# One layer of a four-layer network: from one engine in written order to four, with its works cut into half-unit steps

## The chip, the core and the metric

The kernel runs on one core of a Trainium2 chip. The metric is the device time of one execution in microseconds; the number compared is the median of several runs. The engines are named as in the profile: PE (TensorE, matrix multiplication), DVE (VectorE), ACT (ScalarE), POOL (GpSimd) and SP (the queue that issues transfers). PSUM is the memory that PE writes its results to, in eight banks of 512 float32 per partition. SBUF is the working memory.

## The reference

The reference is a network of four layers over an activation of 8 x 512 x 128 float32. Each layer normalizes `x`, computes a sequence part `s` and a feed-forward part `g`, and adds `s * silu(g)`. Only layer 3 matters here. Its two parts, shortened:

```python
xn = _layernorm(x)
# sequence part: a state-space layer with 4 heads of 64, state size 128
z, x, Bg, Cg, dd_dt, dd_A, trap, angles = split(u @ W_in)
dt = softplus(dd_dt + dt_bias);  adt = min(-softplus(dd_A), -1e-4) * dt
theta = cumsum(angles * dt)
K = rope(rmsnorm(Bg) * B_norm_w + B_bias, theta)
Q = rope(rmsnorm(Cg) * C_norm_w + C_bias, theta)
# chunk by chunk: masked Q K^T with decay, times x; plus a state that is carried on
y = (y_intra + y_inter + D * x) * silu(z)
s = y @ W_out
# feed-forward part: attention of 16 heads of 8, softmax over the queries
scores = einsum('bqd,bkd->bkq', q, k) / sqrt(128)
z = einsum('bkq,bkv->bqv', softmax(scores, -1), v) @ Wo
g = gelu(l2_normalize(l2_normalize(z) @ Wff))
x = x + s * silu(g)
```

## The kernel before

The four layers run one after the other. `x` stays in SBUF. Layer 3 (`layer3`, L1971, and the class `Layer3`, L1593) takes the eight rows of the batch one by one; a row is 512 tokens, that is `JT` = 4 tiles of 128 tokens. Four kinds of work exist for each row, and all but the attention are generators, which are advanced one step at a time up to their next `yield`:

- **A start** (`begin`, L1663, and `parameters`, L1701): normalizes the row (`layernorm`, `rms`), transposes it, projects keys (L1682), queries (L1685, four masked copies at L1688 and L1690) and values (L1694), and then computes everything the state-space part needs for each token: raw B and C and the small parameters (L1713 to L1719), a softplus as a polynomial of some 15 small DVE operations (L1581 to L1590), decays (L1747, L1749), the normalized B and C (L1759), the products of B and C (L1763 to L1774), the angles (L1778 to L1792), sine and cosine (L1795 to L1798).
- **Four mixers** (`mixer`, L1802), one for each tile of 128 tokens: projection of z and x (L1808 to L1814), keys and queries with bias on POOL (L1817), rotation on DVE (L1822 to L1824), the decay matrix (L1829, L1834, masked by POOL at L192), transposes (L1848), the product of keys and queries (L1853, L1854), the carried state (L1859 to L1865), the output (L1870 to L1879), and a transpose of it (L1883, L1884).
- **Sixteen units of attention**: `scores` (L1907) computes four heads for one tile of keys: four matmuls into four PSUM tiles of one bank each (L1916), and for each head a maximum on DVE (L1919) and an exponential with a running sum on ACT (L1920). `weigh` (L1887), two units later (`LAG` = 2), divides the values by the sums (L1893 on DVE, L1894 on POOL) and multiplies them with the exponentials on PE (L1901).
- **A closing** (`end`, L1922): output projections (L1929, L1939), two normalizations, a projection between them (L1955), GELU (L1959) and tanh (L1962), the last products and sum (L1963 to L1966), and one output transfer (L1967).

The loop in `layer3` goes over units. In each unit it issues the scores, advances half of the running works by one step, issues the weighing of two units before, and advances the other half by one step. So each work advances one step per unit. The start of the next row begins at unit 0, a mixer every four units (four units ahead of the row it belongs to), and the closing after the last weighing.

What sets the order: PE executes in the order in which the program is written (`manual_schedule` with PE alone). For DVE, ACT and POOL a scheduler chooses the order from its own estimate of the times and from priorities; `scores` and `weigh` have a higher priority by 300. On every engine the order is fixed once the program is built. Most copies out of PSUM go alternately to ACT and DVE (`evac`, L116 to L122). PSUM holds four banks for scores (`pu`), one for the weighing (`pf`) and three for everything else (`pa`).

Of the kernel before, what the change touches and what calls it, by code (L numbers as in the profile page):

```python
# [20 lines left out]
P = 128  # L21
B = 8
# [1551 lines left out]
def softplus(nc, pool, x):  # L1574
# [5 lines left out]
    nc.scalar.activation(e, e, AF.Exp, scale=-1.0)  # L1580
    nc.vector.tensor_scalar(z, e, 2.0, None, ALU.add)  # L1581
# [11 lines left out]
class Layer3:  # L1593
# [43 lines left out]
    def layernorm(self, x, xn):  # L1637

        k, nc = self.k, self.k.nc
        s1 = self.sp2.tile([P, JT], F32, name="s1")  # L1640
        nc.vector.tensor_reduce(s1, x, AX.X, ALU.add)
        nc.vector.tensor_scalar(s1, s1, 1.0 / C, None, ALU.mult)
        nc.vector.tensor_tensor(xn, x, bc(s1, 2, C), ALU.subtract)
        r = self.rms(xn, JT, 1e-5)
        nc.vector.tensor_tensor(xn, xn, bc(r, 2, C), ALU.mult)

    def rms(self, x, n, eps, floor=False):


        nc = self.k.nc  # L1650
        sq = self.tp.tile([P, n, C], F32, name="sq", bufs=1)
        nc.scalar.activation(sq, x, AF.Square)
        ss = self.sp2.tile([P, n], F32, name="ss")
        nc.vector.tensor_reduce(ss, sq, AX.X, ALU.add)
        if floor:
            nc.vector.tensor_scalar(ss, ss, eps * eps, None, ALU.max)
        else:
            nc.vector.tensor_scalar(ss, ss, 1.0 / C, eps, ALU.mult, ALU.add)
        r = self.sp2.tile([P, n], F32, name="rs")
        nc.gpsimd.tensor_tensor(r, ss, self.k.minus_half.to_broadcast([P, n]), ALU.pow)  # L1660
        return r

    def begin(self, b):  # L1663


        k, nc, cn, fn, tp = self.k, self.k.nc, self.cn, self.fn, self.tp
        bt = slice(b * JT, (b + 1) * JT)
        xn = tp.tile([P, JT, C], F32, name="xn3", bufs=1)
        self.layernorm(self.x[:, bt, :], xn)
# [3 lines left out]
        k.to_features(xn, xT, nt=JT)  # L1673
# [9 lines left out]
        nc.scalar.copy(q["kT"], ps)  # L1683
        ps = k.pa()
# [10 lines left out]
        k.evac(q["V"], ps)  # L1695
# [5 lines left out]
    def parameters(self, q):  # L1701
# [8 lines left out]
        for jt in range(JT):  # L1710
# [9 lines left out]
            if jt % 2:  # L1720
                yield
# [4 lines left out]
        nc.vector.tensor_scalar(beta[:, 0], beta[:, 0], 0.5, 0.5, ALU.mult, ALU.add)  # L1726
        nc.vector.tensor_scalar(beta[:, 1], beta[:, 1], -0.5, 0.5, ALU.mult, ALU.add)
# [4 lines left out]
        softplus(nc, self.sp2, sp.rearrange("p a b c -> p (a b c)"))  # L1732
# [17 lines left out]
        nc.vector.tensor_scalar(flat(v["ell"]), ps[:, 0, :], -1.0, None, ALU.mult)  # L1750
        nc.vector.tensor_tensor(v["eout"], v["eout"], v["c"], ALU.mult)

        r = self.rms(raw.rearrange("p j a n -> p (j a) n"), 2 * JT, 1e-5)
# [3 lines left out]
        for jt in range(JT):  # L1757
            for w in range(2):
                nc.vector.scalar_tensor_tensor(  # L1759
                    BC[:, jt, w, :], raw[:, jt, w, :], rv[:, jt, w : w + 1], nw[:, w, :], ALU.mult, ALU.mult  # L1760
                )
        prod = ap.tile([P, JT, C], F32, name="prod3")
# [12 lines left out]

        W = JT * HM * NA
# [11 lines left out]
        nc.vector.scalar_tensor_tensor(t, n, -TWO_PI[0], theta, ALU.mult, ALU.add)  # L1788
        for part in TWO_PI[1:]:
            nc.vector.scalar_tensor_tensor(t, n, -part, t, ALU.mult, ALU.add)  # L1790
# [6 lines left out]
        nc.scalar.activation(n, n, AF.Square)  # L1797
        nc.vector.tensor_scalar(of(cos), n, -2.0, 1.0, ALU.mult, ALU.add)  # L1798
        q.update(v=v, BC=BC, sin=sin, cos=cos, state=None)
        q["yT"] = tp.tile([P, 2, JT, P], F32, name="yT3", bufs=1)  # L1800

    def mixer(self, b, jt):  # L1802
# [3 lines left out]
        tl = lambda name, *shape: mp.tile([P, *shape], F32, name=name)  # L1806
        ps = k.pa()
# [4 lines left out]
        nc.vector.scalar_tensor_tensor(z, z, 1.0, ps[:, 0:256], ALU.add, ALU.mult)  # L1812
        xv = tl("xv3", HM, HP)
        nc.scalar.copy(xv.rearrange("p h d -> p (h d)"), ps[:, 256:512])  # L1814
        kq = tl("kq3", 2, HM, C)
        bias = cn["kq"].rearrange("p (a h n) -> p a h n", a=2, h=HM)
        nc.gpsimd.tensor_tensor(kq, bc(q["BC"][:, jt], 2, HM), bias, ALU.add)  # L1817
        sn, cs = (bc(q[n][:, jt], 1, 2) for n in ("sin", "cos"))
        x1, x2 = kq[:, :, :, 0:NA], kq[:, :, :, NA : 2 * NA]
        t = [tl(f"rope{i}", 2, HM, NA) for i in range(4)]  # L1820
        for i, (a, r) in enumerate(((x1, cs), (x2, sn), (x1, sn), (x2, cs))):
            nc.vector.tensor_tensor(t[i], a, r, ALU.mult)  # L1822
        nc.vector.tensor_tensor(x1, t[0], t[1], ALU.subtract)
# [8 lines left out]
        E = tl("E3", HM, P)  # L1832
# [3 lines left out]
        xc = tl("xc3", HM, HP)  # L1836
# [3 lines left out]
        if jt < JT - 1:  # L1840
            xe = tl("xe3", HM, HP)
            nc.gpsimd.tensor_tensor(xe, xv, bc(v["eout"][:, jt, :], 2, HP), ALU.mult)
        yield
        kqT = tl("kqT3", 2, HM, C)
        for w in range(2):
# [3 lines left out]
            k.evac(kqT[:, w], ps)  # L1849
# [21 lines left out]
        nc.vector.tensor_tensor(y, y, py[:, 0], ALU.add)  # L1871
        if state is not None:
            for h in range(HM):
                nc.tensor.matmul(py[:, 1, h, :], kqT[:, 1, h, :], state[:, h, :], start=True, stop=True)  # L1874
            inter = tl("inter3", HM, HP)
# [10 lines left out]

    def weigh(self, b, u):  # L1887
# [3 lines left out]
        E, sm = q["held"].pop(u)  # L1891
        heads = lambda a: a.rearrange("p (i v d) -> p i v d", v=4, d=8)[:, :, g, :]
        nc.vector.reciprocal(sm, sm)  # L1893
        nc.gpsimd.tensor_tensor(heads(va[:, kc, 0:C]), heads(q["V"][:, kc, :]), bc(sm, 2, 8), ALU.mult)  # L1894
# [9 lines left out]
        if kc == JT - 1:  # L1904
            k.evac(q["oT"][:, g, :], q["po"].pop(g))

    def scores(self, b, u):  # L1907

        k, nc, q = self.k, self.k.nc, self.q[b]
        g, kc = divmod(u, JT)  # L1910
        E, sm, nm = (self.ep.tile([P, 4, n] if n > 1 else [P, 4], F32, name=nm) for n, nm in ((T, "at3"), (1, "sm3"), (1, "nm3")))
        q["held"][u] = E, sm
        pus = [k.psum("pu", (P, T)) for _ in range(4)]
        for n, pu in enumerate(pus):
            r = slice(n * 32, n * 32 + 32)
# [187 lines left out]
```

## Time and profile before

| what | us |
|---|---|
| median of 3 runs | 3699.23 |
| lowest and highest run | 3694.9, 3702.36 |
| the profiled execution, its own time | 3700.24 |
| its span, first to last instruction | 3698.5 |
| layer 3, from its first matmul to the end of the span (2694.8 to 3698.5) | 1003.7 |
| first exponential of layer 3 (L1920) at | 2730.9 |

The mean granted TensorE clock of the profiled execution is 0.826 of full speed. In a row of the groups, the columns are: line, engine, operation, output and inputs with shapes, count, then busy time in total, mean duration in ns, then the idle time of the engine just before these instructions with what ended most of it. In the timeline a row has start, duration, engine, line, operation, and in brackets the engine's idle time before it with the releaser. PEld is the load of weights, which overlaps PE.

### The profile page before, as it was taken

The page shows a single profiled execution, that of the slowest core. Times are in us where ns is not written, and L with a number is a line of the kernel's source. Part 1 is how long each engine was busy: PE and PEld are TensorE (multiplying, and loading weights), DVE is VectorE, ACT ScalarE, POOL GpSimd, SP SyncE. Part 2 cuts the span into 40 slices and gives each one's busy share as a digit, 9 for nine tenths or more (in the row PEclk, how much of TensorE's full clock was granted, in tenths as well). Part 3 has the DMA queues.
Part 4 walks back from the last instruction along what each step waited for, and adds up shares of the span by engine and source line. Part 5 has one row for each costly group of instructions (what it writes and reads, how often), then busy time and mean ns, then how long its engine had stood idle before and what let it go on. Part 6 is the DMA issues. An engine that isn't in the chain of part 4 may idle for free.

```text
span 3698.5 us, 44947 instructions
## 1 busy us (share of the span) xinstructions
PE 2806.1 (76%) x16390; PEld 1511.0 (41%) x16390; DVE 2297.2 (62%) x6210; ACT 1619.4 (44%) x3150; POOL 788.9 (21%) x919
## 2 busy tenths in 40 slices
PE   6163656510998788699999999998768789887987
PEld 4142434300544444244444444444334444444543
DVE  8889898997573122424345345345467777777775
ACT  5162545401455344333333333333245656666665
POOL 0004040401125665201011111111122222222221
PEclk9585767555789899799998998998878888888987
DMA  3003030302001221100000000000000000000000
GB/s 95 2 2 70 1 80 1 71 2 78 24 2 44 40 40 17 69 1 1 1 1 1 1 1 1 1 1 1 0 21 1 4 4 1 4 4 4 1 4 6
DMA packets 67518, 64.52 MB, mean 17 GB/s; under 512 B 5344, under 2 KB 59616, under 8 KB 66784
## 3 DMA queue, kind: packets, MB, share of 16 engines
q1 hardware_dynamic: 39264, 42.75, 3.8%
q0 software_dynamic: 19712, 14.69, 3.0%
q10 hardware_dynamic: 8320, 4.19, 0.4%
q8 instruction: 129, 2.11, 0.2%
q14 instruction: 93, 0.76, 0.1%
HBM read 43.80 MB, written 17.83 MB: 17 GB/s over the span
## 4 chain that ended last, share of the span: by engine, by line
PE 34%; DVE 17%; ACT 8%; POOL 3%; issue 2%; DMA 0%; POOLq 0%; ACTq 0%; DVEq 0%; SPq 0%
PE pa L1331 6%; PE pu L1349 6%; DVE nm L1919 4%; ACT at L1920 4%; PE pu L1916 2%; DVE mpad L1363 2%; PE pf L1394 2%; PE pf L1901 1%; PE pa L1445 1%; PE pa L1444 1%; PE pa L1829 1%; DVE rope L1822 1%; ACT at L1381 1%; PE pa L1874 1%; PE pa L1468 1%
## 5 line engine op out<-in xcount | busy, mean ns | idle before, releaser
L1920 ACT ACTIVATE at<-pu,nm 128x512 f32<-128x512 f32 x512 | 347.7, 687 | 145.6 <-DVE nm L1919 115.3
L192 POOL TENSOR_SCALAR_AFFINE_SELECT at<-at 128x512 f32<-128x512 f32 x256 | 186.8, 751 | 1034.0 <-ACT at L1381 857.0
L1919 DVE TENSOR_REDUCE nm<-pu 128x1 f32<-128x512 f32 x512 | 326.3, 679 | 66.8 <-PE pu L1916 66.6
L1363 DVE TENSOR_REDUCE mpad<-pu 128x2 f32<-128x256 f32 (+3 forms) x256 | 199.0, 817 | 169.3 <-PE pu L1360 169.3
L1381 ACT ACTIVATE at<-pu 128x1024 f32<-128x1024 f32 (+3 forms) x256 | 171.6, 701 | 286.1 <-PE pu L1349 285.9
L1041 ACT ACTIVATE at<-pu,rsqrt 128x1024 f32<-128x1024 f32 (+3 forms) x256 | 190.2, 791 | 230.3 <-PE pu L1036 227.8
L1916 PE MATMUL pu<-qT,kT 32*128 32x512 f32 x1024 | 247.5, 700 | 6.2 <-ACT at L1920 5.1
L1331 PE MATMUL pa<-hid,f 128*128 128x512 f32 x512 | 222.7, 593 | 0.0
L1349 PE MATMUL pu<-qT,kT 32*128 32x512 f32 (+3 forms) x1024 | 161.4, 518 | 56.3 <-DVE mpad L1363 41.9
L720 PE MATMUL pa<-ident,Y 128*128 128x128 f32 x32 | 7.9, 424 | 216.5 <-DVE Y L711 216.5
L1349 PE MATMUL pu<-kT,qT 32*128 32x128 f32 (+3 forms) x1024 | 152.3, 572 | 14.3 <-ACT at L1381 10.1
L538 POOL DMA_INDIRECT xg<-xn_d,idx x48 | 51.9, 1081 | 511.9 <-PE pf L542 329.5
L1901 PE MATMUL pf<-at,va 128*32 128x512 f32 x1024 | 156.3, 687 | 1.4 <-POOL va L1894 1.4
L1331 PEld LDWEIGHTS pa<-hid,f 128*128 128x128 f32 x512 | 96.6, 190 | 119.5 <-issue 118.9
L1056 PE MATMUL pf<-at,va 128*32 128x512 f32 (+3 forms) x1024 | 107.3, 495 | 45.8 <-POOL at L192 45.5
L1452 DVE SCALAR_TENSOR_TENSOR X<-X,u 128x512 f32<-128x512 f32 x56 | 38.6, 690 | 159.6 <-ACT u L1447 159.6
L1036 PE MATMUL pu<-qT,kT 32*128 32x512 f32 (+3 forms) x1024 | 131.9, 525 | 5.1 <-ACT at L1041 4.4
L1894 POOL TENSOR_TENSOR va<-V,sm 128x32 f32<-128x32 f32 x128 | 38.9, 304 | 449.7 <-DVE sm L1893 404.1
L1349 PEld LDWEIGHTS pu<-qT,kT 32*128 32x128 f32 x1024 | 67.9, 198 | 154.8 <-DVE mpad L1363 115.6
L1916 PEld LDWEIGHTS pu<-qT,kT 32*128 32x128 f32 x1024 | 82.2, 208 | 103.0 <-ACT at L1920 65.2
L979 POOL DMA_INDIRECT f_d<-ys,idx x64 | 101.2, 1580 | 100.4 <-DMA f_d<-ys,idx 64.5
L1332 ACT ACTIVATE hid<-pa,f 128x512 f32<-128x512 f32 x64 | 44.0, 687 | 172.6 <-PE pa L1331 172.6
(596 smaller groups left out, 6609.2 us busy)
## 6 DMA issues: line engine op xcount, KB each, us to landing
w<-in_w_dram SPq DMA_DIRECT2D x24, 512.0 KB, 3.7
f_d<-zeros ACTq DMA_DIRECT2D x8, 512.0 KB, 6.2
xn_d<-xn SPq DMA_DIRECT2D x8, 512.0 KB, 3.5
cmb_f<-f_d SPq DMA_DIRECT2D x8, 512.0 KB, 4.9
w<-in_w_dram SPq DMA_DIRECT2D x16, 256.0 KB, 2.8
w<-in_w_dram SPq DMA_DIRECT2D x24, 128.0 KB, 2.1
f<-in_f_dram SPq DMA_DIRECT2D x1, 2888.0 KB, 12.0
xn<-in_x_dram SPq DMA_DIRECT2D x4, 512.0 KB, 7.3
```

The source lines that it names most:

```text
L192: self.nc.gpsimd.affine_select(a, a if src is None else src, pattern, ALU.is_ge, 0.0, base=0, channel_multiplier=-1)
L1036: nc.tensor.matmul(pu[:, n, 0:m], q["kT"][r, g // 2, kc * P : kc * P + P], q["qT"][r, g, kc * P :], start=True, stop=True,)
L1041: nc.scalar.activation(at_[:, i : i + 2, 0:m], pu[:, :, 0:m], AF.Square, bias=k.rsqrt2, scale=32.0**-0.5)
L1056: nc.tensor.matmul(po[i * 32 : i * 32 + 32, kc * P :], va[:, kc, c0 : c0 + 32], at_[:, i, 0 : T - kc * P], start=(kc == 0), stop=(kc == JT ...
L1331: nc.tensor.matmul(ps, fn[n][:, c0 : c0 + P], src[:, i, :], start=(i == 0), stop=(i == 3))
L1349: self.k.nc.tensor.matmul(pu[:, n, 0:m], a[r, c0 : c0 + P], b[r, q0 : q0 + m], start=True, stop=stop)
L1363: nc.vector.tensor_reduce(top[:, i : i + 2, 16], pu[:, :, 0:m], AX.X, ALU.max)
L1381: nc.scalar.activation(at_[:, i : i + 2, 0:m], pu[:, :, 0:m], AF.Exp, scale=8.0**-0.5)
L1901: nc.tensor.matmul(po[i * 32 : i * 32 + 32, :], va[:, kc, c0 : c0 + 32], E[:, i, :], start=(kc == 0), stop=(kc == JT - 1))
L1916: nc.tensor.matmul(pu, q["kT"][r, kc * P : (kc + 1) * P], q["qT"][r, g, :], start=True, stop=True)
L1919: nc.vector.tensor_reduce(nm[:, w], pu, AX.X, ALU.max, negate=True)
L1920: nc.scalar.activation(E[:, n, :], pu, AF.Exp, bias=nm[:, w], accum_out=sm[:, w])
```

## The change

Layer 3 alone is edited. The parts:

1. `manual_schedule` covers PE, DVE, ACT and POOL; the priorities are gone.
2. The works are cut into more steps, mostly where a value passes from one engine to another, and mixers and starts advance twice per unit (once after the first pair of maxima and exponentials, once after the weighing); closings advance once per unit. The first mixer runs eight steps before the first unit.
3. Scores go into two PSUM tiles of two banks, and one maximum covers two heads. Half of a unit's maxima and exponentials is issued in the first half of the unit, the other half in the second.
4. The division of the values (`scale`) is issued one unit after its scores, and weighing two units after them as before.
5. Alternating copies become fixed to an engine, x is read from an ACT copy of z and x together (`zx3`), most tiles of a mixer have one buffer and `yT3` has two, and each use of the sum of squares has a tile of its own.

The core of the diff:

```diff
-    ctx.enter_context(k.banks("l3p", pu=4, pf=1, pa=3))
+    ctx.enter_context(k.banks("l3p", pu=2, pf=1, pa=3))
-    ctx.enter_context(k.tc.manual_schedule(engines={mybir.EngineType.PE}))
+    ctx.enter_context(k.tc.manual_schedule(engines={E.PE, E.DVE, E.Activation, E.Pool}))
...
+        for _ in range(8):
+            step(mixers)
         for n in range(B * U + LAG):
...
+            next(scores, None)
+            step(mixers)
+            step(starts)
+            next(scores, None)
             if n >= LAG:
+                L.weigh(*divmod(n - LAG, U))
+                if (n - LAG) % U == U - 1:
+                    ends.append(L.end((n - LAG) // U))
+            if 1 <= n <= B * U:
+                L.scale(*divmod(n - 1, U))
+            step(mixers)
+            step(starts)
+            step(ends)
...
     def scores(self, b, u):
-        pus = [k.psum("pu", (P, T)) for _ in range(4)]
+        pus = [k.pu(2) for _ in range(2)]
...
-        for n, pu in enumerate(pus):
-            w = slice(n, n + 1)
-            nc.vector.tensor_reduce(nm[:, w], pu, AX.X, ALU.max, negate=True)
-            nc.scalar.activation(E[:, n, :], pu, AF.Exp, bias=nm[:, w], accum_out=sm[:, w])
+        for i, pu in enumerate(pus):
+            nc.vector.tensor_reduce(nm[:, 2 * i : 2 * i + 2], pu, AX.X, ALU.max, negate=True)
+            for n in (2 * i, 2 * i + 1):
+                w = slice(n, n + 1)
+                nc.scalar.activation(E[:, n, :], pu[:, n % 2, :], AF.Exp, bias=nm[:, w], accum_out=sm[:, w])
+            yield
...
     def mixer(self, b, jt):
-        nc.vector.scalar_tensor_tensor(z, z, 1.0, ps[:, 0:256], ALU.add, ALU.mult)
-        nc.scalar.copy(xv.rearrange("p h d -> p (h d)"), ps[:, 256:512])
+        nc.scalar.copy(zx, ps)
...
+        yield
+        nc.vector.scalar_tensor_tensor(z, z, 1.0, zx[:, 0:256], ALU.add, ALU.mult)
...
             nc.vector.tensor_tensor(t[i], a, r, ALU.mult)
+        yield
         nc.vector.tensor_tensor(x1, t[0], t[1], ALU.subtract)
...
-            k.evac(kqT[:, w], ps)
+            (nc.vector.tensor_copy if w else nc.scalar.copy)(kqT[:, w], ps)
```

In `begin`, `parameters`, `softplus` and `end` the lines are the same but for `yield`s between them, the squares on ACT (`squares`) being issued a step ahead of their sum and root (`root`), and the fixed copies (`turned` takes the place of `to_features`).

## The prediction

> **What bounds the kernel now.** I read the page first, then a table by stretches of time, then, for layer 3 alone (2694 to 3699 us), the groups by line and shape, the list of waits, and the timeline around the longest wait. The change touches nothing before layer 3: in the two built programs the instructions of layers 0 to 2 stand in the same order on every engine.
>
> ```profile
> span 3698.5 us, 44947 instructions
> ...
> L1920 ACT ACTIVATE at<-pu,nm 128x512 f32<-128x512 f32 x512 | 347.7, 687 | 145.6 <-DVE nm L1919 115.3
> ...
> L1919 DVE TENSOR_REDUCE nm<-pu 128x1 f32<-128x512 f32 x512 | 326.3, 679 | 66.8 <-PE pu L1916 66.6
> ...
> L1916 PE MATMUL pu<-qT,kT 32*128 32x512 f32 x1024 | 247.5, 700 | 6.2 <-ACT at L1920 5.1
> ```
>
> The three rows are the loop of the attention part: scores (PE), maxima (DVE), exponentials (ACT), four heads per unit, 16 units per batch row ("row"), eight rows. ACT sat idle 145.6 us ahead of exponentials, mostly for a maximum.
>
> ```profile
> 2850.00:2970.00 120.00, 98.23 (x556) 54.72 (x556) 87.57 (x211) 71.44 (x187) 26.77 (x40) 0.86 0.01 3
> 2970.00:3090.00 120.00, 100.46 (x567) 54.28 (x566) 90.25 (x213) 77.26 (x199) 27.11 (x40) 0.89 0.01 3
> 3090.00:3210.00 120.00, 98.47 (x544) 55.06 (x547) 86.57 (x209) 71.58 (x189) 26.86 (x39) 0.86 0.01 3
> ```
>
> Columns: stretch, its length, busy time of PE, weight load, DVE, ACT, POOL. One row takes 120 us, and no engine is full: DVE 88, ACT 73, POOL 27. PE's 99 is too high, as a matmul held up inside its group counts as busy (one scores group shows 3.16 us in the timeline, a free one 1.14); freely running groups (below) add up to 79. So the order sets the time, not an engine. From the starts of the exponentials I took the length of each unit, a mean over rows 1 to 6, units 0 to 15: 6.9 5.8 6.9 8.4 7.7 10.1 5.8 10.1 17.1 9.4 4.3 4.4 5.5 9.7 4.2 3.9, together 120.0. Units 5 to 9 take 52.5 us. The timeline of row 2 shows why:
>
> ```profile
> 3041.37 3.68 DVE L1759 SCALAR_TENSOR_TENSOR BC<-raw,rs,c 128x128 f32<-128x128 f32 x7
> ...
> 3047.95 0.67 DVE L1788 SCALAR_TENSOR_TENSOR angle<-turns,pa 128x512 f32<-128x512 f32 x1
> 3048.55 0.68 DVE L1966 TENSOR_TENSOR th<-th,x 128x512 f32<-128x512 f32 x1
> 3048.68 2.08 PE L1808 MATMUL pa<-c,xT 128*128 128x512 f32 x2 [9.81 <-DVE angle L1788]
> ...
> 3049.93 0.67 DVE L1854 TENSOR_TENSOR E<-E,pa 128x512 f32<-128x512 f32 x1
> ...
> 3050.80 0.38 ACT L1811 ACTIVATE z<-pa 128x256 f32<-128x256 f32 x1 [7.50 <-PE pa L1808]
> ```
>
> The scheduler laid DVE's parameter and closing work in one piece (3041.4 to 3049.9), ahead of L1788, which frees the PSUM buffer `pa` for PE's next matmul. PE, in written order, stood 9.8 us, and ACT behind it 7.5 us.
>
> [...] 8.5 us of DVE work sat in front of the one instruction PE needed. [...] 679 ns for one bank, and for two banks
>
> ```profile
> L1363 DVE TENSOR_REDUCE mpad<-pu 128x2 f32<-128x1024 f32 x64 | 75.3, 1220 | 41.0 <-PE pu L1360 41.0
> ```
>
> [...] The trace has 1283 ns a load.
>
> **The change part by part.** *Maxima of two banks.* Two reductions of 1.22 replace four; four run back to back in 2.45 us (timeline), two in 2.35, since rows on DVE overlap by about 0.09. That is 0.1 us x 128 units = 13 us of DVE. Against it, the first exponential of a pair waits 1.22 instead of 0.68. Exposed in every unit that would be 0.54 x 128 = 69 us; I take nothing, because the other pair's exponentials (1.33 us) cover it wherever ACT is not starved. Both ends stay in the range.
>
> *Written order and divided works.* Now each half unit holds on each engine one reduction or one pair of exponentials, then one step of the running mixers and starts (closings in the second half only). Steps per unit double, and so do the pieces: a mixer takes nine steps in five units, where it took seven in seven. A piece's consumer on another engine mostly stands half a unit later. Behind the second score pair, which waits on PE for the exponentials of the unit before, stand this half's mixer and start matmuls; behind each reduction on DVE stand the steps of that half. The single buffers (`kq3`, `E3`, `kqT3` and so on) cost nothing: the last read is step 7 at the latest and the next mixer writes them eight steps after. POOL gets the same operations (27.6 us a row, 3.5 in its fullest unit), and SP's eight output transfers stay behind the last `th`; I cost both at nothing, hidden under DVE; uncovered, the longest POOL piece is 2.0 us (L1817), four times a row.
>
> *Small edits.* Evacuations that alternated are now fixed: oT, V, xT go to ACT; zx copies 512 columns rather than 256 (0.2 us x 32 = 7 us of ACT). Table loads in layer 3's order fall from 39 to 30: 9 x 1.283 = 12 us less ACT. All are in the sums.
>
> *The sum.* For each unit I added the work of each engine in the new order. DVE: mean of the row less 0.09; ACT: exponential 0.665 (four in 2.66), copies 0.53 for 512 columns and 0.3 for 256, table load 1.28; PE: a group's start to the next group's when nothing waits (scores 1.06, weighing 1.0, L1829 1.1, L1848 0.6, L1939 3.7).
>
> ```
> unit  0   1   2   3   4   5   6    7   8   9  10  11  12  13  14  15  sum
> PE   3.4 5.7 9.1 7.9 5.2 4.6 5.4  5.8 6.0 3.2 3.3 4.9 3.4 3.2 3.3 4.9 79
> DVE  6.5 3.9 4.4 6.2 5.2 4.4 9.0 11.4 8.2 3.6 4.9 4.6 4.3 3.3 3.1 4.2 87
> ACT  4.3 5.4 5.8 3.5 4.4 6.2 4.8  2.7 7.9 7.9 3.2 2.7 3.8 4.3 3.2 2.7 73
> max  6.5 5.7 9.1 7.9 5.2 6.2 9.0 11.4 8.2 7.9 4.9 4.9 4.3 4.3 3.3 4.9 103.6
> ```
>
> For instance unit 7, DVE: reductions 2.3, eight L1759 at 0.37 = 3.0, mixer steps 6 and 7 2.8, products and sums 1.2, the closing's sum 0.8, small ones the rest. If engines may slip by a unit against each other, a row takes 103.6; in lockstep by half units, the maxima of the 32 halves add up to 114.9. Against 120.0, units 5 to 9 give most: 52.5 to 42.7; units 0 to 4 give 1, units 10 to 15 five. I take the middle, 109.2, because the steps are a half unit apart but PE runs ahead only as far as three `pa` buffers and the score pairs let it.
>
> Six rows: 6 x (120.0 - 109.2) = 65 us less. Row 0: 124.2 before, (92.1 + 103.1)/2 = 97.6 by the same sums, but eight steps of the first mixer now stand ahead of the first scores. After the angle matmuls that chain is, by the same rows: angle work 3.8, table and sines 3.2, cosine to rotated keys 3.1, transposes and copies 2.0, products, state and y 3.4, with handoffs about 16 us in all; net 124.2 - 97.6 - 16 = 11 less. Row 7: 97.9 before, (86.0 + 93.4)/2 = 89.7, 8 less. The closing after the last exponential (25 us) is one serial chain in both orders: nothing. Sum: 65 + 11 + 8 = 84 less. The profiled execution took 3700.2 us (span 3698.5 and 1.7 around it), 1 us above the median 3699.2 of the three runs: 3616 against it, **3615** against the median. What is late next is DVE in units 6 to 8 and PE in 2 and 3.
>
> **The rivals.** *More slip than a unit.* Six rows at 103.6 give 98 less, row 0 124.2 - 92.1 - 16 = 16, row 7 12: 3573; with DVE full all through (87 a row; row 0 81.7, row 7 72.4 on PE) it would be 3450. For it: a heavy DVE stretch follows a heavy PE stretch. Against: they are three units apart, and scores wait for exponentials.
>
> *Lockstep with handoffs, slower.* Every half waits for a late value somewhere, and the wait holds up all behind it in that queue. Place: S, maxima, exponentials and the step behind them. Price: 114.9 and three handoffs of 0.1 us per half (a reduction's end to its exponential measures 0.09) = 124.5 a row: six rows 27 more; row 0 103.1 + 9.6 + 16 = 4.5 more; row 7 5 more; with the total 37 more, 3736. It decides once waits exceed 16 us a row over 103.6, about 1 us a unit. For it: light units (10, 11, 14, 15) already run at 4.2 us, above nothing the new order makes shorter, and the two-bank maximum lengthens their loop. Against: the 17 us unit disappears by construction.
>
> *Given back.* Units 5 to 9 gain ten, light units lose it to the longer loop: 119 to 120 a row, 3690 to 3706. That the order isn't what it says is excluded: the built program has reductions and steps alternating as written.
>
> **How the numbers follow.** Forecast 0.52 (own range 3573 to 3659, the two bounds); more slip 0.12; lockstep, slower 0.28; given back 0.08. A difference under 0.2% (7.4 us) can't be told from no change; of "given back" 0.04 falls there and 0.02 to each side. Faster 0.52 + 0.12 + 0.02 = 0.66, same 0.04, slower 0.30. The range 3550 to 3735 leaves out most of the deeper slip case below and half of the lockstep case above.
>
> **What would show it.** Right: units 5 to 9 near 43 us and no wait of PE for `angle` or `coef` over 2 us; DVE almost full in units 6 to 8; the first exponential some 16 us later after the start of layer 3; the two-bank reduction at 1.22 us; 30 table loads. Wrong: light units above 5 us with ACT waiting on the new maxima, or PE idle ahead of the scores in most units.

## The result and the profile after

| | before | after |
|---|---|---|
| median of 4 runs each | 3697.07 us | 3757.22 us |
| lowest and highest run | 3692.97, 3702.36 | 3750.1, 3765.76 |
| the profiled execution, its own time | 3700.24 us | 3765.76 us |
| first exponential of layer 3 at | 2730.9 us | 2745.0 us |
| length of a row, mean of rows 1 to 6 | 120.0 us | 129.5 us |

The ratio is 1.0163, with a 95% interval of 1.0133 to 1.0193: 1.6% slower, where 2.3% faster was predicted. The page of the kernel after, the rows that answer to the three shown of before (idle time of the engine ahead of them in the last part):

```profile
span 3764.0 us, 45000 instructions
...
L1928 ACT ACTIVATE at<-pu,nm 128x512 f32<-128x512 f32 x512 | 348.6, 689 | 389.8 <-DVE nm L1925 301.3
...
L1925 DVE TENSOR_REDUCE nm<-pu 128x2 f32<-128x1024 f32 x256 | 309.7, 1218 | 105.8 <-PE pu L1921 105.4
L1921 PE MATMUL pu<-qT,kT 32*128 32x512 f32 x1024 | 268.1, 765 | 104.3 <-ACT at L1928 99.4
```

The work is as priced: the maxima take 309.7 us instead of 326.3, the exponentials the same. The waits are not. ACT stands 301.3 us for maxima (115.3 before; all idle time ahead of exponentials is 389.8 against 145.6), PE 99.4 us for exponentials before it may write the next scores (5.1 before).

The units of a row, from the starts of the exponentials as in the prediction:

```
unit      0   1   2   3   4   5    6    7    8    9   10  11  12  13  14   15  sum
before  6.9 5.8 6.9 8.4 7.7 10.1 5.8  10.1 17.1 9.4 4.3 4.4 5.5 9.7 4.2  3.9 120.0
after   6.4 7.0 9.1 8.4 7.9 8.4  10.9 11.3 11.9 8.2 4.5 9.7 5.5 5.4 4.1 10.7 129.5
```

The 17.1 us unit is gone, as the change intends, but its neighbours took most of that back, and units 11 and 15, which have little work, went from about 4 to about 10 us. The timeline of the kernel after shows unit 15 of row 2 (the maximum at 3121.74 is the second one of this unit):

```profile
3118.31 1.13 PE L1921 MATMUL pu<-qT,kT 32*128 32x512 f32 x4 [0.33 <-ACT at L1928]
3119.34 0.69 ACT L1928 ACTIVATE at<-pu,nm 128x512 f32<-128x512 f32 x1 [1.08 <-DVE nm L1925]
...
3119.37 1.16 PE L1875 MATMUL pa<-kqT 128*128 128x128 f32 x8
...
3120.63 0.69 DVE L1876 TENSOR_TENSOR E<-E,pa 128x512 f32<-128x512 f32 x1 [1.39 <-PE pa L1875]
...
3121.40 0.42 DVE L1884 COPY state<-pa 128x256 f32<-128x256 f32 x1
3121.74 1.21 DVE L1925 TENSOR_REDUCE nm<-pu 128x2 f32<-128x1024 f32 x1
...
3123.05 0.69 ACT L1928 ACTIVATE at<-pu,nm 128x512 f32<-128x512 f32 x1 [2.26 <-DVE sm L1938]
...
3124.55 0.30 PEld L1921 LDWEIGHTS pu<-qT,kT 32*128 32x128 f32 x4 [0.93 <-ACT at L1928]
```

The scores of the second pair were ready at 3119.4. DVE took their maximum only at 3121.74, since a mixer step in front of it in the written order (L1876) waited for PE (L1875), which stood behind those scores. Then two exponentials, and only then, at 3124.55, PE's next scores for that pair of banks. It is a closed ring through three queues.

### The profile page after: what moved, and what is told of

Read it like the earlier page. It is cut to its first block, busy times and chain, and to the rows that moved or that the text cites. A ratio compares the mean times of both kernels' runs of the same rounds, so it can differ in the third digit from the quotient of the medians.

```text
span 3764.0 us, 45000 instructions
## 1 busy us (share of the span) xinstructions
PE 2870.8 (76%) x16390; PEld 1529.5 (41%) x16390; DVE 2271.8 (60%) x5934; ACT 1619.8 (43%) x3162; POOL 776.7 (21%) x919
## 4 chain that ended last, share of the span: by engine, by line
PE 49%; DVE 30%; ACT 13%; issue 3%; POOL 3%; DMA 2%; POOLq 0%; ACTq 0%; SPq 0%; DVEq 0%
PE pa L1331 6%; PE pu L1349 6%; ACT at L1928 4%; PE pu L1921 3%; DVE nm L1925 3%; PE pu L1036 2%; PE pa L406 2%; PE pf L1056 2%; PE pf L1952 2%; DVE mpad L1363 2%; DVE Z L674 2%; PE pf L1394 2%; PE pa L1445 1%; DVE Z L680 1%; DVE Z L684 1%
## 5 line engine op out<-in xcount | busy, mean ns | idle before, releaser
L1928 ACT ACTIVATE at<-pu,nm 128x512 f32<-128x512 f32 x512 | 348.6, 689 | 389.8 <-DVE nm L1925 301.3
L1925 DVE TENSOR_REDUCE nm<-pu 128x2 f32<-128x1024 f32 x256 | 309.7, 1218 | 105.8 <-PE pu L1921 105.4
L1921 PE MATMUL pu<-qT,kT 32*128 32x512 f32 x1024 | 268.1, 765 | 104.3 <-ACT at L1928 99.4
L1952 PE MATMUL pf<-at,va 128*32 128x512 f32 x1024 | 178.1, 777 | 0.3 <-POOL va L1939 0.3
L1921 PEld LDWEIGHTS pu<-qT,kT 32*128 32x128 f32 x1024 | 72.0, 214 | 203.6 <-ACT at L1928 187.7
L1036 PE MATMUL pu<-qT,kT 32*128 32x512 f32 (+3 forms) x1024 | 128.9, 514 | 5.7 <-ACT at L1041 4.8
L1349 PEld LDWEIGHTS pu<-qT,kT 32*128 32x128 f32 x1024 | 67.9, 198 | 154.7 <-DVE mpad L1363 115.5
```

The source lines that it names most:

```text
L1036: nc.tensor.matmul(pu[:, n, 0:m], q["kT"][r, g // 2, kc * P : kc * P + P], q["qT"][r, g, kc * P :], start=True, stop=True,)
L1349: self.k.nc.tensor.matmul(pu[:, n, 0:m], a[r, c0 : c0 + P], b[r, q0 : q0 + m], start=True, stop=stop)
L1921: nc.tensor.matmul(pus[n // 2][:, n % 2, :], q["kT"][r, kc * P : (kc + 1) * P], q["qT"][r, g, :], start=True, stop=True)
L1925: nc.vector.tensor_reduce(nm[:, 2 * i : 2 * i + 2], pu, AX.X, ALU.max, negate=True)
L1928: nc.scalar.activation(E[:, n, :], pu[:, n % 2, :], AF.Exp, bias=nm[:, w], accum_out=sm[:, w])
L1952: nc.tensor.matmul(po[i * 32 : i * 32 + 32, :], va[:, kc, c0 : c0 + 32], E[:, i, :], start=(kc == 0), stop=(kc == JT - 1))
```

## The experiments

Each kernel was run in 4 runs or more beside the kernel before on the same chip; the medians of before were 3697 to 3711 us from session to session, so ratios are compared. Row and granted clock are of rows 1 to 6. "Delay" is the median time, in 300 us of the trace, from the start of a run of maxima on DVE to the start of the exponential that ACT held for it; it is good to 0.05 us, which is how far it moves with the rule for where a run begins.

| run | base and edit | us | ratio, 95% interval | row us | clock | delay us |
|---|---|---|---|---|---|---|
| before | | 3697 | 1 | 120.0 | 0.86 | 0.77 |
| after | | 3757 | 1.0163 [1.0133, 1.0193] | 129.5 | 0.80 | 1.31 |
| e1 | after, second score pair late | 3834 | 1.0334 [1.0316, 1.0351] | 136.5 | 0.75 | 1.26 |
| e2 | after, maxima first | 3798 | 1.0229 [1.0212, 1.0246] | 133.1 | 0.79 | 1.31 |
| e3 | after, one-bank maxima | 3728 | 1.0042 [1.0027, 1.0056] | 122.9 | 0.84 | 0.73 |
| e4 | after, only PE written | 3809 | 1.0259 [1.0242, 1.0276] | 133.2 | 0.84 | 1.30 |
| e5 | before, two-bank maxima | 3765 | 1.0170 [1.0150, 1.0191] | 127.3 | 0.82 | 1.31 |
| e6 | after, PE filled | 3791 | 1.0242 [1.0222, 1.0261] | 131.9 | 0.87 | 1.31 |
| e7 | e3, short start | 3721 | 1.0057 [1.0038, 1.0075] | 122.7 | 0.85 | 0.75 |
| e8 | e3, only PE written, priorities | 3822 | 1.0326 [1.0303, 1.0350] | 138.2 | 0.80 | 0.78 |
| e9 | after, four maxima | 3787 | 1.0207 [1.0184, 1.0230] | 132.0 | 0.78 | 1.37 |
| e10 | e3, late maximum | 3797 | 1.0231 [1.0203, 1.0259] | 132.5 | 0.78 | 1.37 |
| e11 | before, two-bank tiles, four maxima | 3786 | 1.0205 [1.0182, 1.0227] | 130.3 | 0.82 | 1.37 |
| e12 | e7, maxima first | 3760 | 1.0131 [1.0108, 1.0155] | 128.5 | 0.81 | 0.78 |
| e13 | e3, spare bank | 3765 | 1.0186 [1.0163, 1.0208] | 130.3 | 0.87 | 0.72 |
| e14 | before, spare bank | 3732 | 1.0090 [1.0068, 1.0112] | 124.5 | 0.85 | 0.77 |
| e15 | after, PE filled a little | 3812 | 1.0316 [1.0288, 1.0345] | 134.5 | 0.81 | 1.31 |
| e16 | before, PE filled | 3700 | 1.0001 [0.9988, 1.0013] | 120.0 | 0.88 | 0.78 |
| e17 | before, constant bias | 3708 | 0.9998 [0.9990, 1.0007] | 120.2 | 0.86 | 0.77 |
| e18 | after, constant bias | 3773 | 1.0170 [1.0153, 1.0187] | 128.9 | 0.81 | 1.31 |

### First round: the ring, the maxima, or the order

Three theories. A: the ring of the timeline above is the loss, and opening it at one place brings the time back. B: the two-bank maximum is the cost. C: the written order of DVE, ACT and POOL is worse than the scheduler's.

*e1*: the matmuls of the second pair move to the second half of the unit, behind PE's steps.

```diff
-        pus = [k.pu(2) for _ in range(2)]
-        for n in range(4):
+        for i in range(2):
+            pu = k.pu(2)
+            for n in (2 * i, 2 * i + 1):
...
```

> The changed kernel with one edit: the matmuls of the second score pair stand in the second half of the unit, just ahead of their maximum, instead of at the head of the unit. Theory A (closed loop): in the changed kernel the second score pair at the unit's head waits on PE for the second exponentials of the unit before, PE's mixer and start matmuls stand behind it, DVE's steps wait for those, and the second maximum stands behind DVE's steps, so a unit is the sum of PE, DVE and ACT pieces. The edit opens this loop: a row falls from 129.5 us to 108 to 116, the total to 3610 to 3670. Theory B (the two-bank maximum is the cost): no change, 3745 to 3765. Theory C (written order on DVE, ACT and POOL is worse than the scheduler's whatever the order): little, 3730 or more.

*e2*: both maxima and all four exponentials ahead of the first half's steps.

```diff
             next(scores, None)
+            next(scores, None)
             step(mixers)
             step(starts)
-            next(scores, None)
```

> The changed kernel with one edit: both maxima and all four exponentials of a unit are issued ahead of the first half's steps, so that no maximum stands behind a step that waits for PE within the same half. Theory A: the loop is opened at its other end, a row takes 110 to 120 us, the total 3630 to 3700. Theory B: no change, 3745 to 3765. Theory C: little, 3730 or more.

*e3*: one-bank score tiles and a maximum for each head, as in the kernel before; all else as after.

```diff
-        pus = [k.pu(2) for _ in range(2)]
+        pus = [k.psum("pu", (P, T)) for _ in range(4)]
...
+            nc.vector.tensor_reduce(nm[:, w], pu, AX.X, ALU.max, negate=True)
+            nc.scalar.activation(E[:, n, :], pu, AF.Exp, bias=nm[:, w], accum_out=sm[:, w])
+            if n % 2:
+                yield
```

> The changed kernel with four one-bank score tiles and four maxima, all else as it is. Theory A: the loop loses the wait for the second head's maximum (1.22 - 0.68 = 0.54 us) in the units that it sets, some 70 to 120 of 128, so 40 to 65 us less: 3690 to 3720, and still well above the kernel in which the loop is open. Theory B: the whole loss comes back, 3680 to 3700. Theory C: 3740 or more, as DVE has 13 us more to do.

*e4*: PE alone in written order, the scheduler for the rest, without priorities.

```diff
-        ctx.enter_context(k.tc.manual_schedule(engines={E.PE, E.DVE, E.Activation, E.Pool}))
+        ctx.enter_context(k.tc.manual_schedule(engines={E.PE}))
```

> The changed kernel with PE alone in written order; DVE, ACT and POOL are ordered by the scheduler, without the priorities of the kernel before. Theory A: the scheduler may lift maxima over waiting steps, which breaks the loop in part, but it may also lay parameter work in one piece again as before: 3680 to 3760. Theory C: back at the time before or faster, 3650 to 3700. Theory B: no change, 3745 to 3765.

A fell as it stood: both ways to open the ring made it slower (1.0334 and 1.0229). e3 gave 1.0042, so 1.2 of the 1.6% come from the two-bank maxima, although the one-bank version has more DVE work (535.98 us of busy time in 738 us of rows, against 515.33 in 777). No order moves between the two: the instructions of layer 3 besides the maxima stand in the same order on DVE in both traces. The page of e3:

```profile
L1925 ACT ACTIVATE at<-pu,nm 128x512 f32<-128x512 f32 x512 | 348.4, 691 | 323.3 <-DVE nm L1924 320.8
...
L1921 PE MATMUL pu<-qT,kT 32*128 32x512 f32 x1024 | 311.6, 742 | 47.7 <-ACT at L1925 47.4
```

The share put down to maxima is even larger here (320.8 us) than in the kernel after (301.3), so it does not tell the two apart. All idle time ahead of the exponentials does: 323.3 us against 389.8.

e4 is slower than after, but it also lacks the priorities of before, so it does not decide on C.

### Second round: each part alone

*e5* is the kernel before with the new `scores` tiles and two-bank maxima alone (the same edit of `scores` as the change's, without the `yield`).

> The kernel before with the two-bank maxima as its only edit: two score tiles of two banks each, a maximum over both banks of a tile, everything else (the scheduler, the priorities, the running order of the steps) as before. Theory B (the coupling of two banks costs the time: the first exponential waits 0.54 us longer for its maximum, and PE waits for two exponentials instead of one before it may issue the next scores): slower by 30 to 60 us, about 3740 to 3770. Theory C (the written order is what makes the kernel after slow, the maxima are harmless by themselves): 3690 to 3715, the 13 us of DVE that they save being little or nothing here. The step of the prediction that is under test took the coupling as covered.

3764.7 us, ratio 1.0170 [1.0150, 1.0191]: as much as the whole loss of the change (1.0163) from this one edit. The scheduler answered the edit with another order, though: of 1167 DVE instructions of layer 3 besides the maxima, 244 fall out of the longest order that the two traces have in common. So e5 alone does not separate the maxima from a new order; e3 and, below, e10 do, where the order is fixed. Its page has the same signature as the kernel after:

```profile
span 3763.1 us, 44828 instructions
...
L1923 ACT ACTIVATE at<-pu,nm 128x512 f32<-128x512 f32 x512 | 347.0, 688 | 245.4 <-DVE nm L1920 225.9
L1920 DVE TENSOR_REDUCE nm<-pu 128x2 f32<-128x1024 f32 x256 | 304.5, 1213 | 62.0 <-PE pu L1916 61.6
...
L1916 PE MATMUL pu<-qT,kT 32*128 32x512 f32 x1024 | 234.0, 739 | 67.6 <-ACT at L1923 66.4
```

ACT's wait for maxima rises by 111 us (225.9 - 115.3) and PE's wait for exponentials by 61 (66.4 - 5.1), for 22 us of DVE work saved (326.3 - 304.5).

*e7*: four steps of the first mixer ahead of the first unit instead of eight (`range(4)`), on e3.

> The kernel after with one-bank score tiles and four maxima (as in the third experiment), and four steps of the first mixer ahead of the first unit instead of eight. The written order puts those steps before the first scores; the first exponentials came 16 us later than in the kernel before. If that start is a plain loss: 5 to 10 us less than with eight steps, about 3720, close to the kernel before (3711 in the last session). If row 0 then has to make up for it, no difference: about 3728.

No difference to e3 (intervals 1.0038 to 1.0075 and 1.0027 to 1.0056). The first exponential came at 2733.6 instead of 2746.8 us, and row 0 took 125.8 instead of 115.6: 10 of the 13 us were given back at once.

*e8*: e3's steps with the scheduling of before, save that the division of the values (`scale`) has no priority; in the kernel before it has it, as part of `weigh`.

```diff
-        ctx.enter_context(k.tc.manual_schedule(engines={E.PE, E.DVE, E.Activation, E.Pool}))
+        ctx.enter_context(k.tc.manual_schedule(engines={E.PE}))
...
+            with k.tc.high_priority(offset=300):
+                next(scores, None)
...
```

> The kernel after with one-bank score tiles, PE alone in written order, and the scores and weighted values at high priority, as the kernel before has them: what is left of the change are its steps (smaller ones, the fixed choice of engine for each copy out of PSUM, the squares and roots taken apart). Theory C (on DVE, ACT and GpSimd the scheduler's order is better than the written one): 3690 to 3715, at or below the kernel before. Theory B (the maxima are the loss, the written order is harmless): the same as with one bank and all four engines written, 3720 to 3735. If the steps themselves are at fault: 3740 or more.

1.0326: C is not borne out, and B's number was wrong too. With these steps the scheduler's order, as e8 sets its priorities, is 15 us a row worse than the written one (138.2 against 122.9); what the missing priority of `scale` costs was not tried. The list of waits of e8 in five and a half rows (total, times, longest) shows heaps of DVE work like the one in the kernel before, only longer:

```profile
ACT at L1925 <- DVE nm L1924: 173.1, 75, 10.4
...
PE pa L1760 <- DVE kqd L1786: 53.3, 5, 10.7
```

So the written order does take such heaps away, but, as far as e8 can tell, it starts from steps that are worse to schedule than those of before. Together the two come to +0.4% (e3).

### Third round: which half of the coupling

A two-bank tile may cost in two ways. B1, late maximum: the first exponential waits for the maximum over both banks. B2, the pair: PE may write a tile only when both its exponentials are done.

*e9* and *e11*: two-bank tiles, but a maximum of its own for each head, in the kernel after and in e5.

```diff
-            nc.vector.tensor_reduce(nm[:, 2 * i : 2 * i + 2], pu, AX.X, ALU.max, negate=True)
+            for n in (2 * i, 2 * i + 1):
+                nc.vector.tensor_reduce(nm[:, n : n + 1], pu[:, n % 2, :], AX.X, ALU.max, negate=True)
```

> The kernel after, its score tiles still of two banks, but with a maximum of its own for each head (four one-bank maxima a unit). The first exponential of a pair then waits 0.54 us less for its maximum; PE still may not write a tile before both exponentials of its pair are done, and DVE has 13 us a row less relief. If the late maximum is what costs (theory B1): most of the 45 us between the kernel after and its one-bank version comes back, 3725 to 3740. If it is PE's wait for the second exponential (theory B2): it stays, 3755 to 3775. Half of each: about 3745.

> The kernel before with score tiles of two banks and four one-bank maxima: the same question on the scheduler's order, where the two-bank maxima alone cost 64 us. B1 (late maximum): near the kernel before, 3695 to 3720. B2 (PE's wait for a pair): 3745 to 3770.

*e10*: one-bank tiles, the two maxima of a pair in reversed order, so that the first exponential needs the second one.

```diff
-            nc.vector.tensor_reduce(nm[:, w], pu, AX.X, ALU.max, negate=True)
+            if n % 2 == 0:
+                for j in (n + 1, n):
+                    nc.vector.tensor_reduce(nm[:, j : j + 1], pus[j], AX.X, ALU.max, negate=True)
```

> The kernel after with one-bank score tiles, and the two maxima of a pair in reversed order: the first exponential waits for the second maximum, about 0.64 us longer, while PE gets its banks back one by one. Theory B1 (late maximum): the loss of the two-bank tiles is back without them, 3755 to 3775. Theory B2 (PE's wait for a pair): as the one-bank version, 3715 to 3730.

(The 13 us of DVE time in the expectation of e9 are of the whole layer, not of a row.) All three lost: 1.0207, 1.0205 and 1.0231. By the times alone e9 and e11 speak for B2 and e10 for B1. The timelines resolve it. First e3, then e10, then e9, each with the two maxima of a pair and the exponential after them:

```profile
3107.37 1.27 DVE L1924 TENSOR_REDUCE nm<-pu 128x1 f32<-128x512 f32 x2
3108.14 0.69 ACT L1925 ACTIVATE at<-pu,nm 128x512 f32<-128x512 f32 x1 [2.51 <-DVE nm L1924]
```

```profile
3136.26 1.28 DVE L1926 TENSOR_REDUCE nm<-pu 128x1 f32<-128x512 f32 x2
3137.80 0.71 ACT L1927 ACTIVATE at<-pu,nm 128x512 f32<-128x512 f32 x1
```

```profile
3139.41 1.28 DVE L1926 TENSOR_REDUCE nm<-pu 128x1 f32<-128x512 f32 x2
3140.95 0.71 ACT L1929 ACTIVATE at<-pu,nm 128x512 f32<-128x512 f32 x1
```

In e3 the exponential starts 0.77 us after the maxima began, as soon as the first is done. In e9 it starts after both, as in e10. The trace shows why: in e9, as in e11, none of the 256 first maxima raises the semaphore that the exponentials wait for; only the second of each pair does. So the exponential was held for every maximum of its pair that stands ahead of it, by a wait that was built into the program. Over 54 such waits in e9 the delay is 1.37 us. So e9 and e11 never took the late maximum away; they are B1 and B2 together, without the DVE time that a two-bank maximum saves. e10 has one-bank tiles and the late maximum alone, in the same order of DVE as e3, and loses 1.9% over e3: 70 us, or 0.55 us for each of 128 units, for a delay some 0.6 us longer. B1 by itself is enough. B2 by itself was not seen in any run. On top of B1 it adds nothing that can be seen: e9, with both, takes 132.0 us a row, and e10, with B1 alone, 132.5.

### Fourth round: the clock, a spare bank, and the maxima off the way

Theory D: the lower granted clock of the kernel after (0.80 in its rows, 0.86 before) is a large part of the loss: PE's slower groups lengthen the ring. That work in PE's pauses would raise the clock was the author's estimate. *e6*, *e15* and *e16* put matmuls with zero weights ahead of the scores, added to an accumulation that is open (256, 96 and 192 columns; in e16 once a unit).

```diff
+    def fill(self):
+        if self.open is not None:
+            for i in range(4):
+                self.k.nc.tensor.matmul(
+                    self.open[i * 32 : i * 32 + 32, 0:256], self.zero, self.cn["zx"][:, 0:256], start=False, stop=False
+                )
```

> The kernel after, with four extra matmuls of zero weights (128x32 by 128x256, added to an open accumulation, so that the sum does not change) on PE ahead of each pair of scores, in three units of four; PE waits there for the exponentials of the unit before. Theory D ([...] the slow groups then lengthen the loop, and this is a large part of the loss): the granted clock of the rows rises from 0.80 to 0.88 or more, the groups of 128x128 matmuls fall towards 1.1 us, and the time falls by 15 to 50 us in spite of the added work, to 3715 to 3745. If the clock is only a by-product of the waits: the clock rises but the time stays or rises, 3755 to 3850, since about 0.5 us a pair is added to PE, at most 12 us a row.

> The kernel after with the zero-weight matmuls of the sixth experiment, 96 columns instead of 256, so that they add about 0.2 us a pair to PE instead of 0.55. If PE's granted clock is a large part of the loss (theory D), it stays near 0.85 and the time falls below the kernel after, 3715 to 3745. If not: 3750 to 3790.

> The kernel before with such zero-weight matmuls of 192 columns ahead of the four scores of a unit, three units in four. Theory D: the granted clock of its rows rises from 0.86 to 0.90 or more and the time falls, 3660 to 3695. If the clock is no limit there, PE has 0.4 us more a unit: 3700 to 3745.

In e16 the clock rose from 0.86 to 0.88 and the time did not move (the scheduler's DVE order moved too, for 110 of 1167 instructions). In e6 it rose to 0.87, above that of before, and the time was 0.8% longer than after. e15 had no rise worth the name (0.81) and was slower still. In these runs a higher granted clock alone didn't bring the time back. How much of the loss the slow groups carry stays open, since the filling itself takes PE time (an estimated 0.5 us a pair in e6, half of the 1.06 us that a weighing with twice the columns, L1952 at 3029.69, takes in the kernel after).

Theory L: the way from the scores through maxima and exponentials to the return of the bank paces the units. *e13* and *e14* give the scores a fifth bank, from the other matmuls (`pu=5, pf=1, pa=2`), in e3 and in the kernel before.

> The kernel after with one-bank score tiles, five banks for them instead of four, and two instead of three for the other matmuls. The first scores of a unit then no longer wait for an exponential of the unit before. If the cycle of scores, maxima, exponentials and the return of the bank paces most units (theory L: every half microsecond on it costs about half a microsecond a unit, as the late maximum and the pair did, each some 70 us alone): a microsecond less on it gives 30 to 90 us, 3620 to 3690. If three banks are needed for the other matmuls, the gain is eaten: 3720 to 3780.

> The same five and two banks in the kernel before, as its only edit. Theory L: 3620 to 3690. If the other matmuls need their third bank: 3710 to 3760.

1.0186 and 1.0090: slower by 1.4% than e3 and by 0.9% than before. By these times the bank that was taken is missed more than the one given helps (in e14 the scheduler's order moved as well), so L was not tested cleanly.

*e17* and *e18* keep the maxima but give the exponential a constant bias; what they leave out is the shift by the maximum.

```diff
-            nc.scalar.activation(E[:, n, :], pu, AF.Exp, bias=nm[:, w], accum_out=sm[:, w])
+            nc.scalar.activation(E[:, n, :], pu, AF.Exp, bias=self.zero, accum_out=sm[:, w])
```

> The kernel before with the exponentials' shift left out: DVE still takes the four maxima of each unit, but nothing reads them, and the exponential has a constant zero as its bias (so the shift by the maximum is the part of the computation that is left out). DVE and PE have the same work as before; from the scores to the return of their bank 0.68 us and a handoff are gone. Theory L (that way paces most units): the reverse of the two-bank edit, which put 0.54 us and an exponential of 0.87 us on it and cost 64 us: 60 to 100 us less, 3600 to 3640. If the way is only felt when it grows: 3680 to 3700. If the order that the scheduler finds is what moves: anything, 3650 to 3750.

> The same in the kernel after: the two-bank maxima are taken as there, nothing reads them, the exponentials' bias is a constant zero (the shift by the maximum is left out). The order of every engine stays as written. What falls away is the wait for the maxima alone, and with it the steps of DVE that the second maximum stands behind; PE still waits for both exponentials of a pair, and for the maximum. Theory L: more than the 60 us that the two-bank tiles cost, 3600 to 3690. If the waits for maxima are slack: 3740 to 3760.

Ratios 0.9998 and 1.0170, each that of its base. These two runs say nothing on L, because the wait that they were to remove is still there. In the lists of waits over the same 695 us, first of the kernel before, then of e17:

```profile
ACT at L1920 <- DVE nm L1919: 68.1, 86, 2.9
```

```profile
ACT at L1922 <- DVE nm L1921: 69.6, 87, 2.9
```

The exponential no longer reads the maximum, but it still waits for DVE's reading of the same tile, with the same delay of 0.77 us. Nearly all exponentials (501 of 512 in the trace) still carry a wait for the semaphore that the maxima raise, so here too the wait is one of the built program.

*e12* aims at something faster: e7 with all maxima and exponentials of a unit ahead of its steps, the edit of e2.

> A try for a faster kernel: one-bank score tiles, four steps of the first mixer ahead of the first unit, and all four maxima and exponentials of a unit ahead of its first half of the steps, so that no maximum stands behind a step that waits for PE (ACT waits for maxima behind such steps for some 200 us of the one-bank version's rows). If that wait is real loss: 3640 to 3700, below both kernels. With two-bank tiles the same edit was slower (1.0229 against 1.0163), because the steps then start later in a unit; if this rules here too: 3730 to 3780.

1.0131, 0.7% slower than e7. ACT's wait for maxima stayed at 205 us in five and a half rows (227.6 in e3). No version beat the kernel before.

## Why the prediction was wrong

Two steps failed. Of the 20.3 us a row between prediction and result, 6.6 are the maxima of two banks, where the runs show the cause; 13.7 are the sum by units, where they show the size and only in part the cause.

**Maxima of two banks: a step that failed, and the one that made the kernel slower.** The prediction put the first exponential's longer wait at 0.54 us, took nothing for it "because the other pair's exponentials (1.33 us) cover it wherever ACT is not starved", and gave 69 us as the upper end. The delay went from 0.77 to 1.31 us, exactly the 0.54. In the kernel before, this edit costs 1.70% of 3700 us, 63 us, after the DVE time it saves. That is 0.49 us for each of 128 units, nearly the upper end. Without the saving (e11: a delay 0.60 us longer, all the DVE work of before) it costs 2.05%, 76 us or 0.59 us a unit. In both of these the scheduler's order moved too, but e10 against e3, where it did not, gives 0.55 us a unit for a delay as long. So on average the delay is exposed nearly in full once in each unit, not in every pair, and not evenly: from before to e11, units change by -3.4 to +3.1 us. The cover wasn't there. In unit 15 above ACT was through with the first pair at 3120.7, and the second maximum began at 3121.74. The prediction's own lines spoke against the cover: ACT already stood 115.3 us for maxima, so it was starved in many units.

**The DVE time saved: not contradicted.** 13 us were counted. The maxima are busy for 16.6 us less (326.3 - 309.7). The kernels with four maxima in two-bank tiles take longer than those with two: e9 than after by 0.44% or 16 us, e11 than e5 by 0.35% or 13 us. But the intervals just overlap, and the delay with four is 0.06 us longer, which at 0.06 us a unit would be up to 8 us of it.

**The sum by units: wrong, by 13.7 us a row.** Predicted 109.2, measured 129.5. Of these 20.3 us, e3 gives back 6.6 (129.5 - 122.9). The other 13.7 are what remains with one-bank maxima: a row then takes 122.9, above "the middle" (109.2) and above the lockstep too (114.9). The slower rival's price, 124.5, is close to it, but it was made for the kernel with two-bank maxima, so the fit is in part luck. What the runs show is where the time lies. The scores were priced at 1.06 us a unit, 136 us for all. In e3 their matmuls are busy for 311.6 us, and PE stands another 47.4 us ahead of them for exponentials, 359 us together, against 252.6 (247.5 + 5.1) before. On the chain of work that ended last (followed back from the last instruction, each time to what released it) they hold 17.1% of rows 1 to 6 in e3 and 7.0% before. So scores do wait for late exponentials, in the place that the rival named; that its handoffs are the cause was not tested. The profile spoke for it in a place that the prediction named and passed over: the light units already ran at about 4 us, with nothing to shorten.

**Units 5 to 9: half right.** The heap is gone, and PE waits for `angle` or `coef` no longer appear among the waits. But the five units went from 52.5 to 50.7 us, not to 42.7. In layer 3's lists of PE's waits, the first two lines are of the kernel before, the third of the kernel after:

```profile
PE pa L1853 <- DVE coef L1773: 40.8, 3, 13.6
PE pa L1808 <- DVE angle L1788: 28.1, 3, 9.8
...
PE pa L1760 <- DVE adt L1751: 35.2, 8, 8.2
```

In these five units PE's idle time fell from 16.5 to 9.8 us a row, while its busy time, in which held matmuls (3.16 us instead of 1.14 in the prediction) and slow ones (2.08 instead of 1.13 below) count, rose from 35.8 to 40.7. DVE's work in units 6 to 8 was priced well (29.1 us, 28.6 in the sum), but these units took 34.1 us. One reading of the stall was off: the 8.5 us of DVE work from 3041.4 to 3049.9 include L1788 itself, at 3047.95, and work behind it; 6.6 us stood ahead of it.

**PE's price of the scores: too low.** A unit's scores were put at 1.06 us, all four heads together. Where PE issues the heads as two pairs, each pair took as long as four heads (1.13 and 1.14 us), here in the kernel after:

```profile
3009.68 1.14 PE L1921 MATMUL pu<-qT,kT 32*128 32x512 f32 x8
...
3032.44 1.13 PE L1921 MATMUL pu<-qT,kT 32*128 32x512 f32 x4
3035.30 2.08 PE L1921 MATMUL pu<-qT,kT 32*128 32x512 f32 x4 [1.73 <-ACT at L1928]
```

(x8 is four heads, two records each.) In the kernel after, all 82 pairs that ran apart at full granted clock took 1.13 us. Pairs don't explain e3 against after, though: e3's scores are busy for longer (311.6 us against 268.1) and e3 is faster.

**PE at full clock: too low in places.** The prediction's PE row takes freely running groups. Over the last line above the granted clock is 0.50, and the group takes 2.08 us instead of 1.13; so it is with L1875 in the kernel after (2.08 us at 3056.17, where the clock is 0.50, and 1.16 at 3119.37, where it is 1.00). In layer 3 of this kernel the clock fell 58 times. What sets off a fall was not shown: the pause ahead of that line was 1.73 us, and over the 3.41 us ahead of a fall (the shortest stretch of one clock in the records) PE was busy for half the time (median 0.52), against 0.86 over the other stretches of this length at full clock. In the runs with filling a higher clock alone didn't bring the time back (0.87 and 3791 us in e6, 0.80 and 3757 us in the kernel after); what the clock carries of the 13.7 us stays open.

**The start: right in size, wrong in meaning.** The first exponential came 14.1 us later (16 predicted), but e7 shows that shortening the start brings nothing. Row 0 took 120.4 us instead of 97.6.

**Row 7 and the table loads: small.** Row 7's fifteen full units went from 93.9 to 91.3 us (8 less predicted; in e3, with one-bank maxima, 86.2, the 8 less). Table loads of layer 3 went from 40 to 32, where the prediction has 39 and 30.

**The sum.** Six rows at 20.3 make 122 us, row 0 another 23, row 7 five, the start two less: 148 of the 150 us between the profiled execution (3765.8) and the 3616 predicted for it.

Of the two signs of being wrong that the prediction named, the first came in two of four light units: 11 and 15 took over 5 us, with ACT waiting for the new maxima. The second nearly came: PE stood ahead of scores in 63 of 128 units.

**What stays open.** Why the one-bank version of the change with all four engines written only comes out level (+0.4%): in e8 the new steps cost about 18 us a row under the scheduler (138.2 against 120.0), of which writing the order regains 15. Which edit of the steps costs that (the smaller pieces, single buffers, fixed engines for copies, or e8's missing priority) was not tried one by one. Nor was PE's wait for a pair tried without the late maximum.

## What to carry to other kernels

A reduction over two tiles at once saved 0.1 us here, but its first consumer started 0.54 us later. Before counting such a saving, look at which engine stands idle ahead of that consumer: if it already waits for this reduction, price the delay, here nearly in full once per unit, and not as covered. When a scheduler chooses the order, an edit can move that order too, so test a step where the order is fixed. When an experiment is to remove a wait, look up the wait in its trace before reading its time; four kernels here looked like evidence and had kept it.

## What the runs showed of the hardware and the program that was not expected

- The scores of two heads, with 32 contraction rows each, took as long as those of four: 1.13 and 1.14 us. So in the kernel after, at full granted clock, a head of a pair that ran apart took twice the time of one of four that were issued together.
- The granted clock is 0.50 or 1.00 in every record of layer 3 in the kernels before and after. It fell to 0.50 58 times in the kernel after and 36 times in the kernel before; the longest pause of PE in the 3.41 us ahead of a fall was 1.50 and 1.90 us in the median.
- An exponential waited for DVE's reading of its PSUM tile although it used nothing that DVE made (69.6 us of waits in e17, 68.1 in the kernel before). It is a wait on a semaphore, set by the built program.
- The busy time of a PE group was no measure of its work here: the same 512 groups of two records for the scores were busy 234.0 us in e5 and 311.6 us in e3.
